# Row normalisation on ScalarE, later edge lists, one more chunk by Strassen, and a regrouped mixing loop in a fused graph layer

## The chip, the cores and the metric

The kernel runs on one core of a Trainium2 chip. The metric is the device time of one execution in microseconds (us). Engines are named as in the profile: PE (TensorE matmuls, PEld its weight loads), DVE (VectorE), ACT (ScalarE), POOL (GpSimd) and SP (SyncE, which here only issues DMAs). All data are fp32.

## The reference

One layer of a graph transformer for N = 10000 nodes with D = 512 features and 160000 edges sorted by destination:

```python
xn  = layernorm(x)                                              # (10000, 512)
gnn = relu(segment_sum((xn @ W)[src] * edge_w, dst) + bias)     # 160000 edges
q, k, v = split(xn @ w_qkv.T)                                   # 8 heads of 64
q = softmax(q, features of a head) * 64**-0.5
k = softmax(k, nodes)
mix = gamma_layernorm((q @ (k.T @ v per head)) @ w_out.T)
x1  = x + gnn + mix
e   = weights of 6 experts, from the mean token (router, top 2 of 11 partitions)
out = x1 + sum_e e * (gelu(layernorm(x1) @ W1[e] + b1[e]) @ W2[e] + b2[e])
```

## The kernel before

The nodes are cut into 20 chunks of 512 rows (128 partitions x 4 rows; the last chunk has 4 x 68). An fp32 matmul of 128x512 shows as two records of the profile.

**Normalised rows.** `normal_rows` loads a chunk of x (SP queue), takes the row statistics on DVE, the inverse root on POOL (`pow`), subtracts and multiplies, and stores the rows to `xn_d` in DRAM (ACT queue). Rows 0 and 2 of each four are done by ACT in two operations, rows 1 and 3 by POOL in one. `work` calls it as PE's planned time goes on, so that all 20 chunks are through within the first `EARLY` chunks of the next stage. At most four chunks are in work beside the two that are kept (`a_io`).

**Keys and queries.** For each chunk: transposed rows `xnT`, key and query products with `wk` and `wq`, exponentials on ACT (scaled by `usable`, a flag that is 1 if the column norms of both weights are small enough to leave out the maxima; `norms` and `as_they_are` compute it in chunk 0), query softmax on DVE, transposed queries stored to `qT_d`, and `G += exp(k).T @ xn`. The first `EARLY` = 3 chunks use plain products (32 matmuls of keys and queries), the others `seven`, a Strassen form with 28 matmuls that needs `kq_sum` and `xs_b`, sums of weights and of rows made by DVE.

**Edges.** After the `EARLY` chunks `place_edges` loads the edge lists (four DMAs on SP) and computes on DVE where each edge falls; then `find_rows` and two flags, `next_nodes` and `oddities`, for a general path that these inputs don't take. 1250 tiles of 128 edges follow. For each, `edges_in` gathers 128 rows of `xn_d` by an indirect DMA that POOL issues (24 buffers, `msg`), and `edges_summed` multiplies them by a selection matrix, windows of 4 or 8 tiles at a time, into a partial row block that ACT copies and stores to `part_d`. `carry` adds sums that cross windows, by DMA. The tiles are spread among the products by `work`: the planned time of a matmul is `PRODUCT` = 0.83 us, and one tile is due every `PACE` = 0.9 us of it. `far_enough` forces tiles where rows of `part_d` are needed by a chunk (`AT_HAND`).

PE's program order is the order of the source (`manual_schedule`). The other engines' queues are ordered by a scheduler, and `behind` pins one instruction after another.

**Between.** The column sums, `general_path` (a branch), the transposes of G, and four pairs of heads: product with the value weights (`pctx`), one forced window of tiles, transpose (`pht`), product with the output weights (`pmix`).

**The loop over chunks.** `attention(c)` loads transposed queries and x, multiplies by the mixed weights (`po`), and normalises. It runs two chunks ahead of the loop. Then `nodes_rows` transposes the gathered sums `at` of chunk c and issues the gather of chunk c+1 (`gathered`); four `pg` products with the graph weights follow, and the results are stored to `x1_d`. After the last gather, POOL loads the expert weights.

**FFN.** The router and the expert products for 20 chunks follow, at nearly full PE use.

Of the kernel before, what the change touches and what calls it, by code (L numbers as in the profile page):

```python
# [17 lines left out]
P = 128  # L18
# [10 lines left out]
EARLY = 3  # L29
ROWS_SOON = 5  # L30
KEPT = 2
PRODUCT = 0.83
PACE = 0.9

# [16 lines left out]
def gps_layer_kernel(  # L51
# [59 lines left out]

    until = const.tile([P, P], F32, name="until")
# [40 lines left out]
    def row_stats(t, r, mv, on_pool=False):  # L153

        st = small.tile([P, SUB, nc.vector.BN_STATS_DIM], F32, name="st")
        for s in range(SUB):
            nc.vector.bn_stats(st[:r, s, :], t[:r, s, :])  # L157
            nc.vector.bn_aggr(mv[:r, s, :], st[:r, s, :])
        ve = small.tile([P, SUB], F32, name="ve")
        nc.vector.tensor_scalar_add(ve[:r], mv[:r, :, 1], EPS)  # L160
        if on_pool:
            nc.gpsimd.tensor_tensor(mv[:r, :, 1], ve[:r], half_neg[:r], ALU.pow)
            return
# [120 lines left out]
    def experts_weights():  # L284
        wp = held_w["pool"] = ctx.enter_context(tc.tile_pool(name="f_w", bufs=1, reuse_waits="tile"))
# [96 lines left out]
    with ExitStack() as ph:  # L382
# [7 lines left out]
        ew = edge_ctx.enter_context(tc.tile_pool(name="edge_w", bufs=3))  # L390
# [6 lines left out]
        norm_ctx = ph.enter_context(ExitStack())  # L397
        tmp = norm_ctx.enter_context(tc.tile_pool(name="edge_t", bufs=1))
        a_io = norm_ctx.enter_context(tc.tile_pool(name="a_io", bufs=4))


        normal = []

        def normal_rows(n):

            for c in range(len(normal), min(len(normal) + n, NCH)):
# [4 lines left out]
                row_stats(xt, r, mv, on_pool=True)  # L411
                minus = small.tile([P, SUB], F32, name="minus")
                nc.vector.tensor_scalar(minus[:r], mv[:r, :, 0], -1.0, None, op0=ALU.mult)
                for i in range(SUB):
                    if i % 2:
                        nc.gpsimd.tensor_scalar(xt[:r, i, :], xt[:r, i, :], mv[:r, i, 0:1], mv[:r, i, 1:2],
                                                op0=ALU.subtract, op1=ALU.mult)
                    else:
                        nc.scalar.activation(xt[:r, i, :], xt[:r, i, :], AF.Identity, bias=minus[:r, i : i + 1])
                        nc.scalar.activation(xt[:r, i, :], xt[:r, i, :], AF.Copy, scale=mv[:r, i, 1:2])  # L420
# [7 lines left out]
        wk = kvp.tile([P, KB, D], F32, name="wk")  # L428
        nc.sync.dma_start(wk, w_qkv_t[:, D : 2 * D].rearrange("(k p) d -> p k d", p=P))
        nc.sync.dma_start(wq, w_qkv_t[:, :D].rearrange("(k p) d -> p k d", p=P))  # L430
        kq_sum = kvp.tile([P, 4, KH, D], F32, name="kq_sum", tag="wv_wo")
# [6 lines left out]
        n_big = ep.tile([1, 2], F32, name="n_big")  # L438
# [3 lines left out]
        def place_edges():  # L442
# [5 lines left out]
            nc.sync.dma_start(row_sb, dst[0:1, :].to_broadcast([P, NET]))  # L448

            nc.vector.tensor_scalar(row_sb, row_sb, 2, None, op0=ALU.arith_shift_right)  # L450
# [7 lines left out]
            nc.vector.tensor_copy(place, dst_sb)  # L458
# [54 lines left out]
        def find_rows(c, other):  # L513

            at = ew.tile([P, 1], F32, name="at")
            lo, hi = span(c)
            past = ew.tile([P, WIDEST], F32, name="past_c", bufs=1)[:, : hi - lo - 1]
# [28 lines left out]
        def edges_in(i):  # L546
# [12 lines left out]
            sel = ew.tile([P, 2 * GROUP, WIN], F32, name="sel", bufs=6)  # L559
# [8 lines left out]
        def edges_summed(i, batch, m, sel):  # L568
# [7 lines left out]
            part = ew.tile([P, D], F32, name="part")  # L576
# [8 lines left out]
        def norms(i, w):  # L585

            sq = b_io.tile([P, KB, D], F32, name="sq", tag="qT")
            nc.scalar.activation(sq, w, AF.Square)
            pn = psum_e.tile([1, D], F32, name="pn", tag="pm")
            for kb in range(KB):  # L590
                nc.tensor.matmul(pn, ones, sq[:, kb, :], start=kb == 0, stop=kb == KB - 1)
            nc.vector.tensor_reduce(n_big[:, i : i + 1], pn, axis=AX.X, op=ALU.max)

        def as_they_are():


            nc.vector.tensor_scalar(n_big, n_big, NORM2, None, op0=ALU.is_le)
            nc.vector.tensor_tensor(n_big[:, 0:1], n_big[:, 0:1], n_big[:, 1:2], ALU.mult)
            pn = psum_e.tile([P, 1], F32, name="pn", tag="pm")
            nc.tensor.matmul(pn, until[0:1, :], n_big[:, 0:1], start=True, stop=True)  # L600
            nc.vector.tensor_copy(usable, pn)

        def oddities():

            n_good = ew.tile([P, 1], F32, name="n_good", bufs=1)
# [3 lines left out]
            n = ew.tile([1, 2], F32, name="n", bufs=1)  # L609
            nc.vector.tensor_scalar(n[:, 0:1], pn, -1.0, float(ALL_GOOD), op0=ALU.mult, op1=ALU.add)  # L610
            nc.vector.tensor_scalar(n[:, 1:2], n_big[:, 0:1], -1.0, 1.0, op0=ALU.mult, op1=ALU.add)
# [10 lines left out]
        def carry_loads(i):  # L622
            on = ew.tile([P, PER, D], F32, name="on", bufs=1)
            nc.scalar.dma_start(on[:CHAINED], by_window[:CHAINED, i * PER : (i + 1) * PER, :])
            own = ew.tile([P, PER, D], F32, name="own", bufs=1)
# [3 lines left out]
        def carry_chained(i):  # L629
            on, own = held.pop("loads")  # L630
            same = ew.tile([P, P], F32, name="same", bufs=1)
# [20 lines left out]
        EARLY_TOTAL = PRODUCT * KB * EARLY * 3 * KB  # L652
# [11 lines left out]
        def work(us):  # L664

            done[1] += us
            if not pools:

                normal_rows(int(done[1] / EARLY_TOTAL * (NCH + 1)) + 2 - len(normal))
                return  # L670
            edges_to(groups_of(int(done[1] / PACE)))

# [130 lines left out]
        def turned_rows(c, xn):  # L803
            xnT = b_io.tile([P, KB, SUB * P], F32, name="xnT")
            transposed(xnT, xn, chunks[c][1], psum, "ps")
            return xnT
# [6 lines left out]

        xn = rows_of(0)
        xnT = turned_rows(0, xn)
        for c, (_, r) in enumerate(chunks):
            if c == EARLY:
                normal_rows(NCH)
                place_edges()
                next_nodes()  # L820
                oddities()
                for soon in range(ROWS_SOON):
                    find_rows(soon, None)
                norm_ctx.close()
                done[1] = -6 * PACE
# [6 lines left out]
            if c < EARLY:  # L832
                for o, w in ((ek, wk), (qt, wq)):
                    sums = []
                    for s in range(SUB):
# [6 lines left out]
                        if c == 0 and o is ek:  # L842
                            norms(0, wk)
                            norms(1, wq)
# [23 lines left out]
            for cb in range(KB):  # L868
# [4 lines left out]
                if c:  # L873
                    added = nc.vector.tensor_tensor(G[:, cb, :], G[:, cb, :], pc, ALU.add)  # L874
                else:
                    nc.vector.tensor_copy(G[:, cb, :], pc)
                work(SUB * PRODUCT)
                if cb == KB // 2 - 1:
                    qT = b_io.tile([P, KB, SUB * P], F32, name="qT")
                    transposed(qT, qt, r, psum, "ps")  # L880
                    nc.scalar.dma_start(qT_d[c], qT[:, :, : SUB * r])
            if c >= ROWS_SOON:
                find_rows(c, added)
            if c == EARLY - 2:
                for inst in sums_for([kq_sum[:, i] for i in range(4)], wk[:, :KH], wq[:, :KH], wk[:, KH:], wq[:, KH:]):
                    behind(inst, added)
# [19 lines left out]
        with ExitStack() as pb:  # L906
# [8 lines left out]
            for cb in range(KB):  # L915
# [9 lines left out]
                edges_to(done[0] + 1)  # L925
                pt = psum.tile([P, P], F32, name="pht", tag="ps")
                nc.tensor.transpose(pt, heads[:, cb, :], ident)
                headsT = tmp.tile([P, P], F32, name="headsT", bufs=2)
                nc.vector.tensor_copy(headsT, pt)
                pm = psum.tile([P, D], F32, name="pmix", tag="ps")  # L930
                nc.tensor.matmul(pm, headsT, wo[:, cb, :], start=True, stop=True)
                nc.scalar.copy(mix[:, cb, :], pm)
        kv_ctx.close()

        done[1] = max(done[1], tiles_of(done[0])[0] * PACE)

# [22 lines left out]
        def gathered(c):  # L959
            r = chunks[c][1]  # L960
            n_rows = far_enough(c)
            at = io.tile([P, SUB, D], F32, name="at")
# [7 lines left out]
        def queries_in(c):  # L970
            qT = io.tile([P, KB, SUB * P], F32, name="qT", bufs=1)
# [14 lines left out]
        def attention(c, beside):  # L986
# [5 lines left out]
            ot = io.tile([P, SUB, D], F32, name="ot", bufs=4)  # L992
# [18 lines left out]
        mixed = [attention(c, lambda: None) for c in range(2)]  # L1011
        for c, (_, r) in enumerate(chunks):
# [3 lines left out]
            def nodes_rows():  # L1016
                transposed(aT, at, r, psum, "ps", by_act=range(KB))
                if c + 1 < NCH:
                    held["at"] = gathered(c + 1)

            if c + 2 < NCH:
                mixed.append(attention(c + 2, nodes_rows))
# [3 lines left out]
            for s in range(SUB):  # L1026
                po = psum.tile([P, D], F32, name="pg", tag="ps")
                times(po, aT, s, r, wg)
                put_out(KB * PRODUCT)
                nc.vector.tensor_tensor(po[:r, :], po[:r, :], bias_b[:r], ALU.add)  # L1030
# [37 lines left out]
    wp, w2_sb, b1_sb, b2_sb, b2_b, rw_sb = (  # L1068
# [342 lines left out]
```

## Time and profile before

| what | us |
|---|---|
| three runs | 3318.09, 3309.79, 3303.76 |
| median | 3309.79 |
| the profiled execution / its span | 3313.32 / 3311.6 |
| first three chunks (plain products) | 0 to 178.8 |
| chunks 3 to 19 by Strassen, with tiles | 178.8 to 1068.3 |
| column sums, branch, heads | 1068.3 to 1117.2 |
| first mixes, to the first transposes of gathered sums | 1117.2 to 1189.3 |
| loop over chunks, to the last such transposes | 1189.3 to 1918.9 |
| the rest, FFN | 1918.9 to 3311.6 |

Read it by stages: the shares of busy time are averages over parts with different limits. A group's line gives line, engine, operation, output and inputs, the number of records, then busy time and mean ns of one, and the idle time before them with what ended it. A line of the timeline gives start and length in us, and in brackets the idle time before it and what released it. A granted clock below 1 (PEclk) means that TensorE ran slower in that stretch.

### The profile page before, as it was taken

What the parts mean: (1) busy time and instruction counts of PE and PEld (TensorE: products, weight loads), DVE (VectorE), ACT (ScalarE), POOL (GpSimd) and SP (SyncE); (2) the same over time, 40 slices, a digit from 0 to 9 for tenths busy, and PEclk for the clock granted to TensorE, in tenths of its full rate; (3) what the DMA queues carried; (4) which work ended last, traced back from release to release, by engine and by line L of the source; (5) the groups of instructions that cost most, each with busy time, mean ns of one, the idle gap of its engine ahead of it and who ended that gap; (6) DMA issues with size and microseconds to landing.
All of it is one profiled execution on the core that took longest, in us unless ns stands there. A gap on an engine that the chain in (4) does not pass through costs nothing.

```text
span 3311.6 us, 36107 instructions
## 1 busy us (share of the span) xinstructions
PE 3206.1 (97%) x12779; PEld 1893.4 (57%) x12779; DVE 1773.9 (54%) x3935; ACT 822.0 (25%) x1664; POOL 1387.6 (42%) x1416
## 2 busy tenths in 40 slices
PE   6999999999999789999999989999999999999998
PEld 3444444444443233333333358888888888888886
DVE  7855556555553256565655666445544455445533
ACT  4422222222221112222222132222222222222211
POOL 6667777777777777777777400000000000000000
PEclk9999999999999999999999989999999999999999
DMA  8778888888878899999999822222121212122111
GB/s 320 286 254 267 273 281 290 283 260 278 277 243 278 295 318 353 340 351 345 341 339 340 246 96 60 56 67 74 51 64 51 89 51 64 51 78 63 52 39 40
DMA packets 216011, 654.39 MB, mean 198 GB/s; under 512 B 34405, under 2 KB 74341, under 8 KB 188107
## 3 DMA queue, kind: packets, MB, share of 16 engines
q0 software_dynamic: 105552, 360.05, 33.7%
q1 hardware_dynamic: 67800, 169.56, 15.5%
q10 hardware_dynamic: 42464, 122.32, 9.5%
q8 instruction: 105, 1.72, 0.2%
q14 instruction: 90, 0.74, 0.1%
HBM read 491.21 MB, written 166.63 MB: 199 GB/s over the span
## 4 chain that ended last, share of the span: by engine, by line
PE 88%; DMA 8%; DVE 2%; issue 1%; POOL 1%; ACT 0%; POOLq 0%; DVEq 0%; SPq 0%; ACTq 0%
PE px L234 15%; PE p L234 12%; PE pz L234 11%; PE py L234 10%; PE pm L574 9%; PE po L200 8%; PE pg L200 8%; PE pc L871 7%; DMA msg<-xn_d,src_sb 4%; PE pt L192 3%; PE ph L234 2%; PE pk L200 2%; DMA xn<-in_x 1%; DMA z_d<-xt 1%; DMA at<-part_d,row_of 1%
## 5 line engine op out<-in xcount | busy, mean ns | idle before, releaser
L556 POOL DMA_INDIRECT msg<-xn_d,src_sb x1250 | 1230.9, 985 | 425.2 <-issue 196.5
L574 PE MATMUL pm<-msg,sel 128*32 128x512 f32 x2504 | 372.6, 603 | 19.4 <-DMA msg<-xn_d,src_sb 17.6
L200 PE MATMUL po<-G,qT 128*128 128x512 f32 (+1 forms) x640 | 297.2, 610 | 18.3 <-DMA qT<-qT_d 18.3
L200 PE MATMUL pg<-wq,aT 128*128 128x512 f32 (+1 forms) x640 | 294.1, 606 | 0.0
L871 PE MATMUL pc<-xn,ek 128*128 128x512 f32 (+1 forms) x640 | 286.4, 596 | 0.7 <-DVE G L874 0.6
L577 ACT COPY part<-pm 128x512 f32<-128x512 f32 x217 | 126.9, 585 | 611.5 <-PE pm L574 603.4
L574 PEld LDWEIGHTS pm<-msg,sel 128*32 128x32 f32 x2504 | 69.1, 109 | 288.1 <-issue 186.3
L200 PEld LDWEIGHTS po<-G,qT 128*128 128x128 f32 (+1 forms) x640 | 116.3, 190 | 186.2 <-issue 162.6
L200 PEld LDWEIGHTS pg<-wq,aT 128*128 128x128 f32 (+1 forms) x640 | 115.5, 188 | 177.1 <-issue 162.2
L234 PE MATMUL px<-xnT,w_sb 128*128 128x256 f32 (+1 forms) x800 | 203.7, 377 | 11.3 <-DVE u L1228 11.1
L157 DVE BATCH_NORM_STATS2 st<-ot 128x6 f32<-128x512 f32 (+1 forms) x160 | 110.2, 689 | 190.8 <-ACT ot L1001 190.2
L871 PEld LDWEIGHTS pc<-xn,ek 128*128 128x128 f32 (+1 forms) x640 | 117.0, 190 | 142.1 <-issue 130.8
L234 PE MATMUL p<-kq_sum,xs_b 128*128 128x512 f32 (+1 forms) x408 | 189.5, 600 | 0.0
L234 PE MATMUL px<-w_sb,hh 128*128 128x256 f32 (+1 forms) x800 | 185.7, 379 | 0.0
L234 PE MATMUL py<-xs,w_sum 128*128 128x256 f32 (+1 forms) x800 | 185.0, 374 | 0.0
L234 PE MATMUL py<-w_sum,hh 128*128 128x256 f32 (+1 forms) x800 | 179.2, 379 | 0.0
L234 PEld LDWEIGHTS px<-xnT,w_sb 128*128 128x128 f32 x800 | 150.4, 191 | 32.7 <-DVE u L1228 13.1
L234 PEld LDWEIGHTS px<-w_sb,hh 128*128 128x128 f32 (+1 forms) x800 | 150.0, 188 | 22.7
L234 PEld LDWEIGHTS py<-w_sum,hh 128*128 128x128 f32 (+1 forms) x800 | 150.0, 188 | 22.7
L234 PEld LDWEIGHTS py<-xs,w_sum 128*128 128x128 f32 x800 | 149.4, 190 | 19.6
L345 ACT ACTIVATE xn<-xn,st_all 128x128 f32<-128x128 f32 x288 | 114.8, 481 | 99.8 <-DMA xn<-x_d 92.1
L234 PEld LDWEIGHTS p<-kq_sum,xs_b 128*128 128x128 f32 (+1 forms) x408 | 73.6, 187 | 109.7 <-issue 84.4
(299 smaller groups left out, 4649.8 us busy)
## 6 DMA issues: line engine op xcount, KB each, us to landing
part_d<-part ACTq DMA_DIRECT2D x217, 256.0 KB
msg<-xn_d,src_sb POOLq DMA_INDIRECT x1250
xn<-in_x SPq DMA_DIRECT2D x19, 1024.0 KB
xn_d<-xn ACTq DMA_DIRECT2D x19, 1024.0 KB
qT_d<-qT ACTq DMA_DIRECT2D x19, 1024.0 KB
qT<-qT_d SPq DMA_DIRECT2D x19, 1024.0 KB
xt<-in_x SPq DMA_DIRECT2D x19, 1024.0 KB
x_d<-ot SPq DMA_DIRECT2D x19, 1024.0 KB
```

Source lines behind the costliest of these rows:

```text
L157: nc.vector.bn_stats(st[:r, s, :], t[:r, s, :])
L192: nc.tensor.transpose(pt[:, s * r : (s + 1) * r], t[:r, s, kb * P : (kb + 1) * P], ident[:r, :r])
L200: nc.tensor.matmul(po[:r, :], t[:, kb, s * r : (s + 1) * r], w[:, kb, :], start=kb == 0, stop=kb == KB - 1)
L234: nc.tensor.matmul(o, lhs[j], rhs[j], start=start and j == 0, stop=stop and j == n - 1, skip_group_check=True)
L345: nc.scalar.activation(xn[:, s, b * P : (b + 1) * P], xn[:, s, b * P : (b + 1) * P], AF.Identity, bias=st[:, b, s, 0:1], scale=st[:, b, s, ...
L556: nc.gpsimd.indirect_dma_start(out=m[k], out_offset=None, in_=xn_d, in_offset=bass.IndirectOffsetOnAxis(ap=src_sb[:, t0 + k : t0 + k + 1], ...
L574: nc.tensor.matmul(pm[h * WIN : (h + 1) * WIN, :], sel[:, k, :], m[k] if k < len(m) else m[0], start=j == 0, stop=j == batch - 1, skip_gro ...
L577: nc.scalar.copy(part, pm)
L871: nc.tensor.matmul(pc, ek[:r, s, cb * P : (cb + 1) * P], xn[:r, s, :], start=s == 0, stop=s == SUB - 1)
```

## The change

- `normal_rows`: one ACT operation (scale and bias) for each of the four rows; POOL adds epsilon, takes the power and makes the bias; no row operation on POOL. Seven buffers instead of four, four chunks ahead instead of two.
- `EARLY` is 2: the third chunk goes by Strassen. All rows are to be through within two chunks. The lists are loaded after the fourth chunk of x, and placed on DVE behind the last row statistics. The two flags come after chunk 5, and the row searches with chunks 5 to 19.
- The squares of the weights are made early, on ACT; the norms are taken by 32 matmuls with one column each, in place of 8 with 512.
- The transposed copies of the first `EARLY` chunks are all on ACT.
- The four head pairs are grouped: all `pctx`, one window of tiles, all `pht`, all `pmix`.
- The loop: a tile is due every 1.03 us (`ROW_PACE`). `attention` runs three chunks ahead (`MIXED`), with two buffers for the queries, five for its result, one for `at`. The gather of chunk c+1 is issued after the third `pg` product of chunk c; for the last three it stays behind the transposes.
- The router's small tiles get a pool of their own.

The diff, cut to its core:

```diff
-EARLY = 3
-ROWS_SOON = 5
+EARLY = 2
+ROWS_IN = 2
+CHECKED = 5
+ROW_PACE = 1.03
+MIXED = 3
...
         ve = small.tile([P, SUB], F32, name="ve")
-        nc.vector.tensor_scalar_add(ve[:r], mv[:r, :, 1], EPS)
+        (nc.gpsimd if on_pool else nc.vector).tensor_scalar_add(ve[:r], mv[:r, :, 1], EPS)
...
-        a_io = norm_ctx.enter_context(tc.tile_pool(name="a_io", bufs=4))
+        a_io = norm_ctx.enter_context(tc.tile_pool(name="a_io", bufs=7))
...
-                row_stats(xt, r, mv, on_pool=True)
-                minus = small.tile([P, SUB], F32, name="minus")
-                nc.vector.tensor_scalar(minus[:r], mv[:r, :, 0], -1.0, None, op0=ALU.mult)
+                last_stats[0] = row_stats(xt, r, mv, on_pool=True)
+                nc.gpsimd.tensor_tensor(mv[:r, :, 0], mv[:r, :, 0], mv[:r, :, 1], ALU.mult)
+                nc.gpsimd.tensor_scalar(mv[:r, :, 0], mv[:r, :, 0], -1.0, None, op0=ALU.mult)
                 for i in range(SUB):
-                    if i % 2:
-                        nc.gpsimd.tensor_scalar(xt[:r, i, :], xt[:r, i, :], mv[:r, i, 0:1], mv[:r, i, 1:2],
-                                                op0=ALU.subtract, op1=ALU.mult)
-                    else:
-                        nc.scalar.activation(xt[:r, i, :], xt[:r, i, :], AF.Identity, bias=minus[:r, i : i + 1])
-                        nc.scalar.activation(xt[:r, i, :], xt[:r, i, :], AF.Copy, scale=mv[:r, i, 1:2])
+                    nc.scalar.activation(xt[:r, i, :], xt[:r, i, :], AF.Identity,
+                                         bias=mv[:r, i, 0:1], scale=mv[:r, i, 1:2])
...
-            nc.vector.tensor_scalar(row_sb, row_sb, 2, None, op0=ALU.arith_shift_right)
+            behind(nc.vector.tensor_scalar(row_sb, row_sb, 2, None, op0=ALU.arith_shift_right), last_stats[0])
...
-            pn = psum_e.tile([1, D], F32, name="pn", tag="pm")
-            for kb in range(KB):
-                nc.tensor.matmul(pn, ones, sq[:, kb, :], start=kb == 0, stop=kb == KB - 1)
-            nc.vector.tensor_reduce(n_big[:, i : i + 1], pn, axis=AX.X, op=ALU.max)
+            pn = psum_e.tile([P, KB], F32, name="pn", tag="pm")
+            for cb in range(KB):
+                for kb in range(KB):
+                    nc.tensor.matmul(pn[:, cb : cb + 1], sq[:, kb, cb * P : (cb + 1) * P], ones,
+                                     start=kb == 0, stop=kb == KB - 1)
+            nc.vector.tensor_scalar(small_norms[:, i], pn, NORM2, None, op0=ALU.is_le)
...
-        EARLY_TOTAL = PRODUCT * KB * EARLY * 3 * KB
+        pace = [PACE]
+        EARLY_TOTAL = PRODUCT * KB * ROWS_IN * 3 * KB
...
-                normal_rows(int(done[1] / EARLY_TOTAL * (NCH + 1)) + 2 - len(normal))
+                normal_rows(int(done[1] / EARLY_TOTAL * (NCH + 1)) + 4 - len(normal))
...
-            transposed(xnT, xn, chunks[c][1], psum, "ps")
+            transposed(xnT, xn, chunks[c][1], psum, "ps", by_act=range(KB) if c < EARLY else (1, 3))
...
+        squared = [squares_of(wk, "qT"), squares_of(wq, "xs_b")]
+        kq_sum = kvp.tile([P, 4, KH, D], F32, name="kq_sum", tag="wv_wo")
+        normal_rows(2)
+        lists = edges_listed()
...
                 normal_rows(NCH)
-                place_edges()
-                next_nodes()
-                oddities()
-                for soon in range(ROWS_SOON):
-                    find_rows(soon, None)
+                place_edges(*lists)
                 norm_ctx.close()
-                done[1] = -6 * PACE
+                pools["w"] = edge_ctx.enter_context(tc.tile_pool(name="edge_w", bufs=3))
+                done[1] = -16 * PACE
...
-                edges_to(done[0] + 1)
+            edges_to(done[0] + 1)
+            headsT = tmp.tile([P, KB, P], F32, name="headsT")
+            for cb in range(KB):
                 pt = psum.tile([P, P], F32, name="pht", tag="ps")
                 nc.tensor.transpose(pt, heads[:, cb, :], ident)
-                headsT = tmp.tile([P, P], F32, name="headsT", bufs=2)
-                nc.vector.tensor_copy(headsT, pt)
+                nc.vector.tensor_copy(headsT[:, cb], pt)
+            for cb in range(KB):
                 pm = psum.tile([P, D], F32, name="pmix", tag="ps")
...
-        done[1] = max(done[1], tiles_of(done[0])[0] * PACE)
+        pace[0] = ROW_PACE
+        done[1] = tiles_of(done[0])[0] * ROW_PACE
...
-            at = io.tile([P, SUB, D], F32, name="at")
+            at = io.tile([P, SUB, D], F32, name="at", bufs=1)
...
-            qT = io.tile([P, KB, SUB * P], F32, name="qT", bufs=1)
+            qT = io.tile([P, KB, SUB * P], F32, name="qT")
...
-            ot = io.tile([P, SUB, D], F32, name="ot", bufs=4)
+            ot = io.tile([P, SUB, D], F32, name="ot", bufs=MIXED + 2)
...
-        mixed = [attention(c, lambda: None) for c in range(2)]
+        mixed = [attention(c, lambda: None) for c in range(MIXED)]
...
                 transposed(aT, at, r, psum, "ps", by_act=range(KB))
-                if c + 1 < NCH:
+                if NCH > c + 1 >= NCH - MIXED:
                     held["at"] = gathered(c + 1)
-            if c + 2 < NCH:
-                mixed.append(attention(c + 2, nodes_rows))
+            if c + MIXED < NCH:
+                mixed.append(attention(c + MIXED, nodes_rows))
...
                 put_out(KB * PRODUCT)
+                if s == SUB // 2 and c + 1 < NCH - MIXED:
+                    held["at"] = gathered(c + 1)
```

## The prediction

> **What bounds it now.** The profiled execution took 3313.32 us: a span of 3311.6 and 1.7 around it, 3.5 above the median of 3309.79. I read the slices first.
>
> ```profile
> PE 3206.1 (97%) x12779; PEld 1893.4 (57%) x12779; DVE 1773.9 (54%) x3935; ACT 822.0 (25%) x1664; POOL 1387.6 (42%) x1416
> ...
> PE   6999999999999789999999989999999999999998
> ...
> POOL 6667777777777777777777400000000000000000
> PEclk9999999999999999999999989999999999999999
> DMA  8778888888878899999999822222121212122111
> ```
>
> PE looks full, but a busy stretch also covers short waits between the matmuls of an edge tile. Next the costliest groups, for what POOL does.
>
> ```profile
> L556 POOL DMA_INDIRECT msg<-xn_d,src_sb x1250 | 1230.9, 985 | 425.2 <-issue 196.5
> L574 PE MATMUL pm<-msg,sel 128*32 128x512 f32 x2504 | 372.6, 603 | 19.4 <-DMA msg<-xn_d,src_sb 17.6
> L200 PE MATMUL po<-G,qT 128*128 128x512 f32 (+1 forms) x640 | 297.2, 610 | 18.3 <-DMA qT<-qT_d 18.3
> ```
>
> A gather costs POOL 0.985 us and 0.30 to the next. The matmuls of a tile cost 2 x 0.298 at this mean, though an undisturbed window of 8 tiles is 1.86 (0.233 a tile): the rest is waiting. The timeline of PE inside the loop over chunks shows it.
>
> ```profile
> 1580.15 1.04 PE L574 MATMUL pm<-msg,sel 128*32 128x512 f32 x2
> 1582.09 1.05 PE L574 MATMUL pm<-msg,sel 128*32 128x512 f32 x2 [0.90 <-DMA msg<-xn_d,src_sb]
> 1583.43 1.04 PE L574 MATMUL pm<-msg,sel 128*32 128x512 f32 x2 [0.29 <-DMA msg<-xn_d,src_sb]
> 1585.55 1.04 PE L574 MATMUL pm<-msg,sel 128*32 128x512 f32 x2 [1.07 <-DMA msg<-xn_d,src_sb]
> ```
>
> So from about 950 us on the gathers set the pace. A loop chunk without waits is 37.5 us with 28 tiles (1507.0 to 1545.4 less 0.9); from the first transposes of gathered rows (1189.3) to the fifteenth (1753.0) 14 chunks took 563.7, or 40.3. POOL issued 457 operations in 600 us of loop, 1.31 each; 29 tiles and the other POOL work of a chunk fill those 40. The waits view and the timeline at the start give the other stalls.
>
> ```profile
> PE po L200 <- DMA qT<-qT_d: 18.3, 2, 9.2
> PE pt L192 <- ACT xn L420: 12.5, 1, 12.5
> PE pn L600 <- DVE n_big L598: 9.2, 1, 9.2
> ...
> 173.84 1.26 POOL L556 DMA_INDIRECT msg<-xn_d,src_sb  x1 [8.83 <-DMA xn_d<-xn]
> ```
>
> The last line is the first gather: it waits for the last store of normalised rows. From 173.8, 1250 gathers and about 50 other POOL transfers at 1.27 to 1.31 end at 1825 to 1877; the last edge work ended near 1870. The edge stream, not PE alone, decides when the loop ends. The FFN (1918.9 to 3311.6) is not touched.
>
> **Start.** Rows: POOL loses two row operations of 2.14 a chunk (38 in 81.1 us) and gets three small ones; DVE loses `minus`, 0.18. ACT has four operations a chunk before (two on each even row, 0.71 each) and four after, one a row: no ACT time is added. Seven buffers and four chunks of lead let loads start earlier. Before, the 20 loads ran to 154, 7.7 us apiece. In these windows (PE, PEld, DVE, ACT, POOL, clock, DMA share, GB/s)
>
> ```profile
> 20.00:40.00 20.00, 18.00 (x41) 6.41 (x40) 11.72 (x39) 10.42 (x13) 18.51 (x12) 1.00 1.01 424
> 40.00:60.00 20.00, 10.85 (x20) 4.20 (x19) 15.52 (x40) 7.25 (x12) 12.01 (x8) 0.74 0.60 241
> 100.00:120.00 20.00, 20.00 (x60) 9.72 (x59) 20.00 (x108) 10.73 (x18) 14.43 (x9) 1.00 0.69 217
> 140.00:160.00 20.00, 20.00 (x48) 8.78 (x47) 13.31 (x30) 7.69 (x12) 11.29 (x6) 1.00 0.53 213
> ```
>
> the DMA engines are full only at 20 to 40 and idle for half of 140 to 160. Loads and stores of rows (20.5 MB each), weights (2.1), edge lists (2.6) and vectors (0.8) make 46.6 MB: 116 us at 401 GB/s (80 to 100), 152 at the mean 307 of the first 160. I take the last row landing at 108 to 111, the last store and first gather at 130, 44 earlier than now.
>
> What it costs is order. ACT now copies chunk 0's transposes behind the rows of x0 to x3 and both weight squares. x3 arrives after 4.1 MB of rows, 2.1 of weights and the vectors, near 22; statistics 3.0, POOL about 2.5, four rows 2.9 and copies 2.4 put the first key matmul near 33 (18.7 now). Its 32 records take 16.9, not 13.9, after an idle stretch, as a 52.44 us record of now shows (clock 0.74 in that slice). The norms become 32 matmuls of one column: by the row of column sums (four in 0.95) 7.6 us instead of 7.2, and waits of 2.0 and 9.2 behind them. But `usable` now stands on DVE behind the statistics of x2 to x10, and all exponentials, and PSUM space for the query matmuls, wait for it. x10 arrives near 60, so `usable` at 62 to 66 (52.5 now). Chunk 1 starts near 98 (86.5), transposes of chunk 2 near 125. Then one DVE queue holds, directly behind the last statistics, the placing of the edges (19 us), two copies, the query softmax of chunk 1 and the four weight sums (5.2): about 25 us to the transposed queries of chunk 1, at 150, and 10 more for these and the second half of its context matmuls. Chunk 2 starts at 161; now at 133.8. **+27**, between +7 (queues cost only the initial 14, part of it won back) and +66 (below).
>
> A rule speaks against rows on ACT: the Trainium skill, "ScalarE: Activation LUTs", Rules for kernel authors, sends add and multiply to VectorE. The row here says otherwise: ACT takes 0.71 for 128x512, and DVE is busy all of 100 to 120, with the queue that sets chunk 2. By the rule 80 row operations would join that queue, some 53 us of DVE by its 0.67 for the same shape read by the statistics; I stay with the rows.
>
> **Keys phase.** Chunk 2 by Strassen has 28 matmuls instead of 32: 3.4 saved at 0.858. From chunk 2's start to the column sums is 934.5 now (133.8 to 1068.3); after: -3.4, +7.4 for 32 more tiles (712 summed by then, not 680), and -12 of waits for gathers near 966 and 1042 to 1064, since the stream has 44 us of lead. **-8**.
>
> **Transition.** Five forced windows of eight tiles lie between general path and first mix, all waiting for gathers in part, with a chain transpose, copy, matmul per head pair. After: one window before them, and the four transposes and four products grouped. Now 48.9 (1068.3 to 1117.2); after 4.8 branch, 3.7 transposes, 1.9 + 1.9 for two windows, 4.3 context, 1.7 head transposes and copies, 4.4 products: 23. **-26**; the tiles are counted where they go. If the gathers have no lead, half returns.
>
> **First mixes.** Query loads with one buffer stopped PE twice (18.3) and left slow records, about 6:
>
> ```profile
> 1142.41 6.08 PE L200 MATMUL po<-G,qT 128*128 128x512 f32 x8 [9.21 <-DMA qT<-qT_d]
> ```
>
> Two buffers cover the load: a wait of 9.2 fits under the 13.7 of the products of the chunk before. Three chunks go ahead, so 16 more matmuls (13.7) stand before the first transposes and not later. 60 matmuls at 0.858 and 48 tiles at 0.235 make 63.5, against 72.1 for 44 matmuls, waits and tiles. **-9** to the first transposes (1189.3 now; 1173 after), now with 776 tiles done, not 760.
>
> **Loop.** A pace of 1.03 instead of 0.9 gives 26 tiles a chunk. PE then needs 37.0; POOL's 27.7 operations at 1.31 need 36.3. 14 chunks x (40.3 - 37.0): **-46**; if the stream stays at 38.5 a chunk, -25. What is not done in these chunks remains: 116 tiles must be summed before the rows of chunks 15 to 18, in runs of 20, 28, 32 and 20 tiles with little product work between. They come at 1.25 to 1.31 each; from the fifteenth transposes to the last edge work 143 instead of 117.6: **+25**. Half of the loop's gain is so given back. The gathers of node rows now start in the middle of the products and have one buffer; their 7 us is covered by the 3.4 to 17 us of work before the transposes. The tail after the last edge work keeps its weight loads, 48.3.
>
> **Sum.** +27 - 8 - 26 - 9 - 46 + 25 = -37. Cross-check by the stream: first gather 44 earlier and 1.31 each gives at most -44, reduced by the loop's PE time. I take -34: 3279 for this execution, 3276 by the median.
>
> **Rivals.** *Queues at the start hide* (0.17): DVE places edges while PE still has chunk 1, because x19 arrives by 100; chunk 2 starts at 141, and 20 more are won: 3257. For it: DVE has 5 to 8 us free in most windows; against: 100 to 120 has none. *Gathers go on setting the loop* (0.17): DMA share is 0.95 to 0.99 in it, and POOL's 1.31 may be the transfers' rate; 38.5 a chunk returns 21, and 3297 is left. *Row loads do not speed up* (0.13, slower): x goes on landing every 7.7 us, because stores and loads share engines that reach 1.01 in one window. Then x10 lands near 76 and x19 at 154; `usable` and the edge placing, which now stand behind them on DVE, move with them, the first gather stays at 174 and chunk 2 starts near 200: 39 more than forecast, and the stream's lead is lost too. 3318 to 3328. It decides from a start of chunk 2 at 197.
> *Earlier gathers do nothing*, because PE sets the keys phase anyway: that is the 12 of the sum there, and lies inside the range.
>
> **Chances.** The forecast has 0.53. A measurement tells about 0.5%, 16.5 us. Faster than 3293: most of the forecast, the first rival, and a third of the second: 0.73. Within: most of the second, the edge of the forecast: 0.17. Slower: the third with its worse end: 0.10. Range 3244 to 3312: lower end the first rival with 13 for the loop's waits, upper end between the second and third.
>
> **What would show it.** Right: first gather near 130; chunk 2's first Strassen matmul near 160; no `qT` wait at the first mixes; loop chunks of 37 with few waits for `msg`; a run of waits for `msg` before the last four transposes. Wrong: a first gather at 170, loop chunks of 39 or more, or end runs as long as all that was saved.

## The result, and the profile after

The changed kernel took 3317.18 us (median), the kernel before 3310.11 beside it: a ratio of 1.002, interval [1.0012, 1.0028]. So it is 7 us slower, where 34 fewer were forecast. The profiled execution after has a span of 3316.1 us.

The page after, the lines that answer to those of before:

```profile
PE 3179.8 (96%) x12819; PEld 1906.1 (57%) x12819; DVE 1777.0 (54%) x3902; ACT 834.6 (25%) x1674; POOL 1329.2 (40%) x1437
...
PE   5699999999999999999998879999999999999998
...
POOL 2367777777776777777777400000000000000000
PEclk8899999999999999999999989999999999999999
DMA  9568888888888999999998822122121212122111
...
L557 POOL DMA_INDIRECT msg<-xn_d,src_sb x1250 | 1238.3, 991 | 438.2 <-issue 211.6
L575 PE MATMUL pm<-msg,sel 128*32 128x512 f32 x2504 | 339.6, 603 | 10.7 <-DMA msg<-xn_d,src_sb 6.9
```

POOL's digits begin late, at 2 and 3: the row operations are gone, yet the 7s of the gathers start in nearly the same slice. They end in the same slice. PE has lower digits in slices 22 to 24 (8, 8, 7; before 9, 9, 8), at the end of the loop. The waits of PE say what they are, after and then, in the last line, before:

```profile
PE pt L198 <- DMA at<-part_d,row_of: 35.5, 4, 11.7
PE pt L198 <- ACT xn L421: 13.9, 4, 13.2
PE pk L206 <- ACT xnT L200: 13.3, 1, 13.3
...
PE pt L198 <- DVE xnT L200: 12.0, 2, 6.9
PE pt L198 <- DVE qt L191: 8.2, 3, 5.5
PE pm L575 <- DMA msg<-xn_d,src_sb: 6.9, 7, 2.2
...
PE pt L192 <- DMA at<-part_d,row_of: 6.0, 1, 6.0
```

The 18.3 for transposed queries is gone and waits for messages fell from 17.6 to 6.9. In their place stand 35.5 for the gathered sums (6.0 before) and, at the start, waits for ACT and DVE; of these the first (13.9) was there before, with 12.5.

By stages, from the timelines of PE (us):

| stage | before | after | change | forecast |
|---|---|---|---|---|
| start of chunk 2 | 133.8 | 175.0 | +41.2 | +27 |
| from there to the column sums | 934.5 | 932.2 | -2.3 | -8 |
| to the first mix | 48.9 | 23.4 | -25.5 | -26 |
| to the first transposes of gathered sums | 72.1 | 68.9 | -3.2 | -9 |
| fourteen chunks | 563.7 | 515.6 | -48.1 | -46 |
| to the last transposes | 165.9 | 204.2 | +38.3 | +25 |
| the rest | 1392.7 | 1396.8 | +4.1 | 0 |
| sum | 3311.6 | 3316.1 | +4.5 | -37 |

The last row is not the change: in a later profile of the same kernel the rest took 1391.7.

What ties these rows together is the stream of gathers. Its first, 24th, 25th and 49th gathers after the change, on POOL's timeline, then the 51st and the last:

```profile
153.84 2.16 POOL L557 DMA_INDIRECT msg<-xn_d,src_sb  x1 [11.95 <-DMA xn_d<-xn]
...
189.15 1.19 POOL L557 DMA_INDIRECT msg<-xn_d,src_sb  x1 [0.30 <-issue]
200.45 0.94 POOL L557 DMA_INDIRECT msg<-xn_d,src_sb  x1 [10.11 <-PE pm L575]
...
235.75 0.95 POOL L557 DMA_INDIRECT msg<-xn_d,src_sb  x1 [4.36 <-PE pm L575]
238.57 1.03 POOL L557 DMA_INDIRECT msg<-xn_d,src_sb  x1 [0.30 <-issue]
...
1856.23 0.95 POOL L557 DMA_INDIRECT msg<-xn_d,src_sb  x1 [0.30 <-issue]
```

The 25th, the 51st and the last before:

```profile
204.83 0.95 POOL L556 DMA_INDIRECT msg<-xn_d,src_sb  x1 [0.30 <-issue]
237.48 1.11 POOL L556 DMA_INDIRECT msg<-xn_d,src_sb  x1 [0.30 <-DMA msg<-xn_d,src_sb]
1857.52 0.94 POOL L556 DMA_INDIRECT msg<-xn_d,src_sb  x1 [2.27 <-DMA msg<-xn_d,src_sb]
```

The first gather is at 153.8 instead of 173.8. But at 200.45 the 25th waits 10.1 us for PE to free the first of 24 buffers, and at 235.75 another waits 4.4. Counted from zero, gather 50 starts at 238.6 (237.5 before), gather 600 at 944.0 (944.7), gather 1000 at 1504.5 (1503.9), and the last at 1856.2 (1857.5). The last tile is summed at 1869.1 and was at 1870.1. At these places the change moved the stream by 1.3 us at most, and nowhere from the 50th gather on by more than 5.4, though PE's stages before and after differ by up to 48 us. From 300 to 1000 us POOL hardly waits for PE. Its lines there for its own issue and for the buffers, after (total, times, longest):

```profile
POOL msg L557 <- issue: 86.2, 283, 0.3
...
POOL msg L557 <- PE pm L575: 16.1, 53, 0.3
```

So none of these waits is longer than the 0.30 that stands between any two gathers.

### The profile page after: what moved, and what is told of

Its sections match the earlier page's. It is cut to its first block, busy times and chain, and to the rows that moved or that the text cites. A ratio compares the mean times of both kernels' runs of the same rounds, so it can differ in the third digit from the quotient of the medians.

```text
span 3316.1 us, 36159 instructions
## 1 busy us (share of the span) xinstructions
PE 3179.8 (96%) x12819; PEld 1906.1 (57%) x12819; DVE 1777.0 (54%) x3902; ACT 834.6 (25%) x1674; POOL 1329.2 (40%) x1437
## 4 chain that ended last, share of the span: by engine, by line
PE 55%; DMA 8%; DVE 1%; issue 1%; POOL 1%; ACTq 0%; ACT 0%; POOLq 0%; DVEq 0%
PE px L240 14%; PE pz L240 10%; PE py L240 9%; PE po L206 7%; PE pg L206 7%; PE pm L575 4%; DMA msg<-xn_d,src_sb 3%; PE ph L240 2%; DMA z_d<-xt 2%; DMA xt<-x_d 1%; PE pt L198 1%; DMA at<-part_d,row_of 1%; POOL msg L557 0%; DVE xt L1314 0%; DMA w_sb<-in_w 0%
## 5 line engine op out<-in xcount | busy, mean ns | idle before, releaser
L575 PE MATMUL pm<-msg,sel 128*32 128x512 f32 x2504 | 339.6, 603 | 10.7 <-DMA msg<-xn_d,src_sb 6.9
L206 PE MATMUL po<-G,qT 128*128 128x512 f32 (+1 forms) x640 | 288.8, 599 | 0.0
L240 PE MATMUL p<-kq_sum,xs_b 128*128 128x512 f32 (+1 forms) x432 | 200.7, 600 | 0.0
```

The lines of the kernel that those rows point to most:

```text
L206: nc.tensor.matmul(po[:r, :], t[:, kb, s * r : (s + 1) * r], w[:, kb, :], start=kb == 0, stop=kb == KB - 1)
L240: nc.tensor.matmul(o, lhs[j], rhs[j], start=start and j == 0, stop=stop and j == n - 1, skip_group_check=True)
L575: nc.tensor.matmul(pm[h * WIN : (h + 1) * WIN, :], sel[:, k, :], m[k] if k < len(m) else m[0], start=j == 0, stop=j == batch - 1, skip_gro ...
```

## The experiments

Theory S: the stream sets the time of the last tile, from its 25th gather on; PE time that is saved becomes waiting for it, late or early. Rival P: PE's own work and order set the time, and the gains and losses of its stages simply add up. In the profiles of the 18 runs with all gathers the span ends 1441 to 1454 us after the start of the last tile, while that start lies anywhere from 1848 to 2171. So the question is what sets the last tile.

The runs fall into two kinds by the chip that they were on. On one kind the kernel before takes about 3311, on the other (three chips) 3569 to 3576, and there only ratios are used. Whether it is the chip or what else ran on it then, no run tells.

**First windows sooner.**

```diff
-                done[1] = -16 * PACE
+                done[1] = -6 * PACE
```

> The changed kernel with the first tiles due 6 instead of 16 places after the start of the edge work. Theory S (the stream of gathers on POOL sets the end of the loop from its 25th gather on; it started 20 us earlier after the change, then stood 10.1 us at its 25th gather and 4.4 at a later one, until PE had freed a buffer): both waits shrink to under 2 us, the gathers from the 50th on run 10 to 14 us earlier than in the changed kernel, the last tile is summed near 1857 instead of 1869.6, and the time is 3303 to 3307. Rival P (PE's own work and order set the time: the start lost 41 us and the rest won that back): the same tiles are only summed earlier, 3314 to 3320.

3311.88 us, 1.0002 [0.9991, 1.0012] of the kernel before. The changed kernel did not run beside it; its two measurements on this kind of chip are 3317.18 and 3315.09, so 3 to 5 more, and the second has an interval that overlaps this one. The wait at the 25th gather fell to 0.92, gather 50 starts at 222.0 (16.6 earlier), gather 800 at 1203.0 (21.3 earlier), the last tile is at 1860.2 (8.9 earlier). S has the direction and the stream right. The time lies between the two ranges, 5 above that of S and 2 below that of P: 12 us of the lead were lost again in the last 400 gathers.

**The loop alone on the kernel before.** The loop and the heads of the change, as in the diff above, put into the kernel before.

> The kernel before with the loop of the change (pace 1.03, three chunks ahead, two query buffers, gathers of sums in mid-products) and the grouped heads, and the start left as it was. Theory S: heads and first mixes are some 35 us shorter and loop chunks 37 instead of 40, but the last tile is summed at 1865 to 1875 as before, the waits for messages move to the last chunks, and the time is 3307 to 3318. Rival P, by the terms of the prediction (-26 heads, -9 first mixes, -46 loop, +25 end): 3250 to 3262.

3357.77 us, 1.0144 [1.0123, 1.0166]: both theories missed. The stages did shrink (first transposes at 1159.6 instead of 1189.3), and the stream kept its times to gather 950 (1434.8, 1435.4 before). Then the runs of put-off tiles begin, three chunks earlier than in the changed kernel. PE's waits in this kernel, then POOL's from 1160 to 1900:

```profile
PE pt L194 <- DMA at<-part_d,row_of: 68.8, 7, 11.9
```

```profile
POOL msg L558 <- PE pm L576: 67.6, 60, 15.4
```

After each run PE stands for the last part's store, the carry and the gather of sums. Meanwhile the buffers fill and POOL stands too (67.6, against 22.4 before in the same stretch). So the stream itself is stopped by the runs, and the last gather is 40 us later, at 1897.7. S had taken the stream as unable to get slower; it holds only while PE frees the buffers in time.

**Half the gathers**, in both kernels (two tiles share a gathered block, the sums are not the reference's):

```diff
+                        if k % 2:
+                            m[k] = m[k - 1]
+                            continue
                         m[k] = pools["m"].tile([P, D], F32, name="msg")
```

> The kernel before, with every second gather of edge rows left out (two tiles share one gathered block, all matmuls stay; so the edge sums are not the reference's). Theory S: the waits for messages go: 12 us at the end of the keys phase, about 12 in the heads, 36 in fourteen loop chunks and 8 after them, so 3235 to 3255. Rival P: only the measured waits of 17.6 go, 3290 to 3300.

> The changed kernel with the same gathers left out (so the edge sums are not the reference's). Theory S: the runs of tiles before the last chunks go at PE's 0.235 a tile, the time is 3275 to 3295, and so the change is 30 to 50 slower than before once the stream does not hide it: its start is 41 later and its PE savings are small. Rival P: 3300 to 3315, within 10 of the kernel before with half its gathers.

3241.51 for the kernel before and 3269.04 for the changed one (one run each). So gathers at the full number cost the kernel before about 70 us and the changed one about 48. At half of them the change is 27.5 slower: its first transposes are at 1182.4 against 1156.8, the loss of the start. 16.9 of waits for gathered sums stay even so; the chain after a run is real. P's ranges are missed by 48 and 31. S has the kernel before within its range, and the changed one 6 below it.

**Four kernels on a chip of the other kind.** The pace alone, the row loads, three plain chunks, and two of these with a still earlier first window:

```diff
-ROW_PACE = 1.03
+ROW_PACE = 0.9                       # loop_pace_09
...
+            if c + 1 == EARLY:       # row_loads_first
+                normal_rows(NCH)
...
-EARLY = 2
+EARLY = 3                            # three_plain_chunks
...
-                done[1] = -16 * PACE # start_and_pace: with row_loads_first and ROW_PACE = 0.93
+                done[1] = -2 * PACE
```

> The changed kernel with one tile due every 0.9 us in the loop, as before, instead of every 1.03. Theory S with the late chain (the pace of 1.03 only puts tiles off; each run of them before one of the last chunks then ends in a part store, a carry and a gather of sums, 25 us with PE mostly idle): loop chunks of 39 to 40, no long runs of tiles at the end, the waits for gathered sums fall from 35.5 to under 12, the last tile is summed at 1862 to 1870, and the time is 8 to 14 below the changed kernel, 3303 to 3309. Rival P (the loop's saving is real work saved): fourteen chunks cost 40 more and the end gives 30 to 38 back, 3318 to 3328.

> The changed kernel with the last two row loads put on the SP queue ahead of the reload of chunk 2's rows (which waits there for PE until 104). The last row lands near 112 instead of 126, edges are placed from 116 instead of 130, the first gather is at 140 to 144 and chunk 2 starts at 162 to 166 instead of 175. Theory S: what counts is the first freed buffer, 10 earlier; so the last sum is 5 to 10 earlier and the time 3307 to 3313. Rival P: all 10 to 13 of the start are won, 3304 to 3307. If the queue was not what held the start, no change: 3317.

> The changed kernel with the third chunk plain again (edges begin with chunk 3; the rows still go through within two chunks). PE no longer waits for the weight sums and the placing in chunk 1, so chunk 3 starts near 195 to 200 instead of 216, but the first tiles are due there and not in chunk 2. Theory S: the first window is summed near 220 instead of 201, the stream and the last sum are 15 to 20 later, and the time is 3325 to 3337. Rival P: the start is 15 to 20 shorter on PE and that stays: 3297 to 3304.

> The changed kernel with the row loads first, tiles due 2 places after the start of the edge work, and a pace of 0.93 in the loop. Theory S: first window near 180, the gathers 20 earlier than in the changed kernel, the last sum 1845 to 1852, no long runs, 3285 to 3295. Rival P: 3304 to 3320.

0.9894 [0.986, 0.9928], 0.9881 [0.9834, 0.9929], 1.0154 [1.0124, 1.0184] and 0.9926 [0.9902, 0.9951] of the kernel before. No changed kernel ran beside them. Three plain chunks is the clear one. Its column sums are at 1217.1, where the two kernels with the unchanged window offset have 1251 and 1253 (with 672 tiles summed by then, not 712, which is some 9 us of the difference at 0.235 a tile). It is still 95 to 97 us slower than these. Its POOL timeline shows why:

```profile
235.18 0.95 POOL L557 DMA_INDIRECT msg<-xn_d,src_sb  x1 [50.49 <-PE pm L575]
```

The first gathers were as early as ever, and the 25th waited 50.5 us for PE. That is S against P: PE was ahead and the time was lost all the same. The loss is larger than S had said, since the runs also came earlier, as in the loop experiment.

Row loads first did not do what its edit was meant to do. In SP's timeline the reload of chunk 2 (105.99) still stands ahead of the last two loads; only the last rows' statistics and operations moved ahead of chunk 1's other work. Chunk 2 started at 168.0, not 162 to 166, and the first gather at 148.6.

**The pace beside the changed kernel**, again on that kind of chip:

> The changed kernel itself, as the measure for the three beside it on the same chip. Both theories: within 0.4% of the kernel before where the gathers go at 1.28 us each in the keys phase, as in the first profiles; on a chip where they go slower (1.49 in the four runs before this one) theory S expects a different ratio, since the first wait and the end of the stream then weigh more.

> The changed kernel with a tile due every 0.9 us in the loop instead of 1.03. Theory S with the late chain: chunks of 39 to 40, no long runs at the end, waits for gathered sums under 12 instead of 35.5, last tile summed within 8 of the changed kernel's, time 8 to 14 below it. Rival P: 5 to 10 above it.

> The kernel before with the loop and heads of the change, but with a tile due every 0.9 us. Theory S: the 46 that the same kernel lost at a pace of 1.03 were put-off tiles (122 left at the fifteenth chunk, 69 of waits for gathered sums); at 0.9 the stream sets the loop (39.5 to 40.5 a chunk), the last tile is at 1858 to 1868, and the time is 3300 to 3310, 0 to 10 below the kernel before. If three chunks ahead or the grouped heads themselves did the harm, it stays above 3335. Rival P: 3270 to 3285.

> The changed kernel with the first tiles due 6 places after the start of the edge work and a pace of 0.92 in the loop. Theory S: the two gains add (stream 9 earlier at its end, and the waits for gathered sums shorter by 20 or more): last tile at 1852 to 1860, 3296 to 3304, faster than both kernels by 0.2% or more. Rival P: 3312 to 3325.

0.9971 [0.994, 1.0002], 0.9945 [0.9921, 0.9968], 0.9924 [0.9895, 0.9953] and 0.9937 [0.9912, 0.9962]. The first two profiles show what the pace does to the changed kernel: fourteen chunks take 572.6 at 1.03 and 644.3 at 0.9, the rest to the last transposes 220.5 and 150.7. The sums are 793.1 and 795.0; the last tile is at 2120.5 and 2122.3. The loop's 72 us are put off and come back, as S says. The shorter waits for gathered sums were to win 8 to 14, as I had added to S; the medians are 6 apart, with overlapping intervals, so that is not shown. The kernel before with the loop at 0.9 is not slower than before, so three chunks ahead and the grouped heads did not cause the 46 of the earlier run; on one chip the two paces were not compared for it. As ratios, S had expected it at 0.997 to 1 and P at 0.988 to 0.992: 0.9924 lies between, nearer to P, on a kind of chip for which neither was worked out.

A second round of these on that kind of chip:

> The changed kernel with a tile due every 0.9 us in the loop. On a chip with gathers at 1.28 us, theory S with the late chain: chunks of 39 to 40, waits for gathered sums under 12 instead of 35.5, 3303 to 3311, 6 to 14 below the changed kernel. Rival P: 3320 to 3328. On a chip with gathers near 1.5 (kernel before near 3570): loop chunks of 44 to 46, 0 to 0.5% below the changed kernel's 0.997 of before.

> The kernel before with the loop and the heads of the change at 0.9 us a tile. On a chip with gathers at 1.28, theory S: 3300 to 3312, against 3357.8 with the pace of 1.03; if three chunks ahead or the heads did that harm, over 3335; rival P: 3270 to 3285. On a slow chip: 0.99 to 0.995 of before.

> The changed kernel with the first tiles due 6 places after the start of the edge work and a pace of 0.92. On a chip with gathers at 1.28, theory S: last tile 1852 to 1860, 3296 to 3304. Rival P: 3312 to 3325. On a slow chip: 0.99 to 0.995 of before.

> The changed kernel with the last row loads ahead of the reload on SP, the first tiles due 2 places after the start of the edge work, and a pace of 0.93. On a chip with gathers at 1.28, theory S: first window near 181, last tile 1845 to 1852, 3290 to 3298, the fastest of the four. Rival P: 3305 to 3320. On a slow chip: 0.985 to 0.993 of before.

0.9903 [0.9871, 0.9936], 0.9942 [0.9922, 0.9962], 0.9919 [0.9897, 0.9941] and 0.9926 [0.9897, 0.9955]: all 0.6 to 1% below the kernel before, and not told apart. The last three lie in the ranges given for such a chip, the first 0.002 below its own.

**The earliest stream beside the changed kernel**, on the first kind of chip:

> The changed kernel as the measure for the run beside it: 1.000 to 1.004 of the kernel before on a chip with gathers at 1.28 us in the keys phase, 0.993 to 1.001 on one with gathers near 1.5.

> The changed kernel with the last row loads first, tiles due 2 places after the start of the edge work and a pace of 0.93. Theory S: the first window 18 to 20 earlier than in the changed kernel, the last tile 12 to 25 earlier, and the time 0.4 to 0.8% below the changed kernel on either kind of chip (3290 to 3302 on the first kind). Rival P: within 0.2% of it.

The changed kernel: 3315.09 us, 1.0012 [1.0001, 1.0024]. With the same early call for the last rows (their loads again behind the reload, at 105.84), the first windows 14 places sooner and a pace of 0.93: 3298.1 us, 0.9955 [0.9939, 0.997], 17 below the changed kernel and 13 below the kernel before. Its POOL timeline at the 25th gather, and PE's wait for gathered sums:

```profile
180.44 0.95 POOL L557 DMA_INDIRECT msg<-xn_d,src_sb  x1 [0.30 <-issue]
181.97 0.94 POOL L557 DMA_INDIRECT msg<-xn_d,src_sb  x1 [0.58 <-PE pm L575]
```

```profile
PE pt L198 <- DMA at<-part_d,row_of: 2.8, 1, 2.8
```

The wait of 9.5 in the changed kernel beside it is 0.58 here. Gather 50 is 19.6 earlier (216.4 and 236.0), gather 600 16.5, the last 23.4 (1833.2 and 1856.6), the last tile 21.5, the last transposes 18.9. A lead that is won by the 50th gather is still there 1200 gathers later. The first window is summed 15.9 earlier, where S had 18 to 20; the last tile and the time are in its ranges, and P's 0.2% is missed. Three things are changed at once here. First windows sooner changed the lead alone: it moved the last tile by 8.9 and the time by less than is clear of noise, and lost 12 of its lead at the pace of 1.03. That the smaller pace kept the lead here fits, but how much of the 17 is the pace was not separated on this kind of chip.

## Why the prediction was wrong, by its steps

**The lead of the stream** is the step that failed. I read rightly that the edge stream decides when the loop ends, and then put its start at the first gather: 44 us earlier, so at most 44 won. The first gather came 20 earlier, at 153.8 and not at 130, and of these 20 nothing was left at the 50th. Two things were left out. The lead is limited to 24 buffers, and the change itself makes the first tile due 16 places after the start of chunk 2 instead of 6 after chunk 3. PE summed the first window at 199.1 (194.5 before). I had that line of the diff before me and costed only what PE would do later. With the lead gone, PE savings between 240 and 1857 could not bring the last tile forward. In the sum that is the loop's -46, right at -48.1 as a stage and worth nothing, because the stream's last gather stayed. Of my three signs of being wrong none came up (a first gather at 170, chunks of 39, where they took 36.8, or end runs as long as all that was saved): they watched the first gather and the stages, not the 25th gather.

In the sum by stages the misses are start 14, keys 6, first mixes 6, end 13 and the rest 4, less 2 in the loop: the 41.5 between -37 and +4.5.

**The start** was sized at +27 and is +41.2, and the same delay puts off the first window. I let the last row land at 108 to 111. In SP's timeline of the changed kernel the reload of chunk 2's rows, which waits 14.6 us for PE, stands ahead of the last two loads:

```profile
104.24 0.33 SPq L807 DMA_DIRECT2D xn<-xn_d  x1
104.67 2.47 SPq L415 DMA_DIRECT2D xn<-in_x  x2
```

The last statistics start at 126.5, the placing of edges at 130.0, and the two DVE copies of chunk 2's rows (6.95 and 5.03 of PE idle) and the query softmax of chunk 1 (5.49 and 2.08) stand in that same queue. The chain was the one I described; its head was some 15 later. PE itself came to chunk 2's transposes at 131.5, 6 later than the 125 of the sum. No run had the loads ahead of the reload, so what that order alone cost is not measured. My remark that DVE is full from 100 to 120, taken from before, no longer held (PE, PEld, DVE, ACT, POOL, clock, DMA share, GB/s; after):

```profile
100.00:120.00 20.00, 20.00 (x48) 8.81 (x47) 6.80 (x18) 13.98 (x21) 1.75 (x5) 1.00 0.97 375
```

DVE waits there for rows. The load that the change took off POOL is now on ACT, whose row operations take 0.805 instead of 0.714, so "no ACT time is added" was off by 0.09 a row. The Trainium skill, "ScalarE: Activation LUTs", What ACT_TABLE_LOAD costs, states about 93 ns more for each pointer operand; an estimate from its figures gives 0.71 with one pointer and 0.80 with two, as measured. No run here moved the rows to DVE, so its rule that I set aside stays untested. My price for it, 0.67 a row, was that of the statistics; in this trace a DVE operation with one tensor and a constant takes 0.60 for 128x866 (133.60), so 53 us was probably too much.

**Transition and heads**: -25.5 for -26, each term near its row. **Keys**: -2.3 for -8; a wait of 1.14 is left, and two windows of eight tiles took 5.65 (at 1058.89) and 4.61 (at 1092.70) instead of 1.92. These 6.4 are short waits inside them; POOL had stood 7.95 for a carry at 1058.55. **First mixes**: the query waits went as forecast, but 48 tiles took (68.9 - 51.5) / 48 = 0.36 each, not 0.235: two windows (3.57 at 1162.22, 5.17 from 1172.78) waited for gathers, since there was no lead, and the others took 0.24 to 0.27 a tile. (My 63.5 there should be 62.8, and the "2 x 0.298" of a tile is 0.298; neither changes a term.)

**The end** was +38.3 for +25. The step "their 7 us is covered by the 3.4 to 17 us of work" took only the gather of sums. In PE's timeline after (the last run of tiles before chunk 16's rows, then the transposes of chunks 16, 17 and 19):

```profile
1779.50 12.30 PE L575 MATMUL pm<-msg,sel 128*32 128x512 f32 x28 [2.19 <-DMA msg<-xn_d,src_sb]
1791.73 3.70 PE L206 MATMUL pg<-wq,aT 128*128 128x512 f32 x8
1795.27 10.46 PE L206 MATMUL po<-G,qT 128*68 128x512 f32 x24
1817.30 3.68 PE L198 MATMUL pt<-ident,at 128*128 128x128 f32 x16 [11.57 <-DMA at<-part_d,row_of]
...
1861.01 3.68 PE L198 MATMUL pt<-ident,at 128*128 128x128 f32 x16 [6.10 <-DMA at<-part_d,row_of]
...
1919.33 2.04 PE L198 MATMUL pt<-ident,at 68*128 68x68 f32 x16 [11.71 <-DMA at<-part_d,row_of]
```

From the end of the run (1791.8) it takes 25.5 us to the transposes: the carry is issued at 1797.5, and the gather behind it at 1810.4. 14 of these are covered by products, 11.6 are not. I had left 48.3 for the tail after the last edge work, which holds such a chain, and did not carry the chain to the other chunks. On POOL, the carry and the gather of sums for chunk 16, then the gather for chunk 18, when the edge gathers are over:

```profile
1797.53 0.99 POOL L647 DMA_DIRECT2D part_d<-part_d  x1
...
1810.44 0.94 POOL L984 DMA_INDIRECT at<-part_d,row_of  x1 [0.30 <-issue]
...
1883.26 1.06 POOL L984 DMA_INDIRECT at<-part_d,row_of  x1 [4.10 <-DMA part_d<-part_d]
```

Between the first two, 12.9 apart, POOL issued eight edge gathers. The third comes 5.7 after its carry (1877.57). So up to 7 us of the chain may be the order of POOL's queue and not the transfers; no run changed that order.

The rival of slow row loads was on the right side for a wrong reason: loads did speed up, yet the placing of edges stood behind the last of them, and the stream gained nothing. Of the other rivals, the queues at the start did not hide (chunk 2 at 175.0, not 141), and the loop's chunks took 36.8 and not 38.5: the gathers' limit came out at the end of the loop.

## What to carry to other kernels

Where a bounded ring of buffers feeds an engine, the lead of the producer starts when the consumer frees its first buffer, not when the first transfer starts: look for both in the trace, and count items against time in the two kernels rather than add stages. If two stages change by tens of microseconds and the n-th item comes at the same time, that stream is the likely bound, and work taken out of the consumer is only put off; halving the items, as here, is a test of it. Putting work off to the last moment also lengthens the end by the whole chain behind it, and can stop the stream in turn.

## What the hardware showed that I had not expected

Some of POOL's small operations stretched: a power on 128x4 took 7.06 us at 129.99 (1.04 mostly), while DVE placed the edges, and a gather 4.97 at 165.99 (0.95), while DVE made sums of rows and selection matrices. The power was on the way to the last store of rows, and so to the first gather. The Trainium skill, "GPSIMD Engine Reference", Specifications, says that POOL shares its SBUF interfaces with DVE and that they contend when a DVE instruction is in a 2-port mode or reads two SBUF inputs; DVE ran back to back in both stretches, many of its operations with two inputs. No run tested it.

On the second kind of chip the kernel before is 8% slower, the part after the last gathered sums is not (1394.5 in the changed kernel there). Between 300 and 1000 us the gathers' median spacing is 1.25 us there as well, but the mean is 1.55 instead of 1.28: 39 gaps over 2 us, where the first profile after has none. PE, ACT and DVE also show waits of several us for their own issue. POOL's waits there, of the changed kernel in that stretch:

```profile
POOL msg L557 <- issue: 100.1, 322, 0.9
POOL msg L557 <- PE pm L575: 95.3, 45, 10.9
POOL msg L557 <- remote: 28.2, 23, 3.4
```

What stops the engines there is open. The ratio of the same two kernels moved from 1.002 to 0.997 with it.
